# Attention and MLP layers on one core: the second attention's q and k by seven block products, and its fillers in a new order

## The chip, the cores and the metric

The kernel runs on one core of a Trainium2 chip. The metric is the device time of one launch in microseconds (us), inputs and outputs in device memory.

## The reference

Sixteen images of 256 channels and 1024 pixels, all in float32, pass through two layers:

```python
# layer 0: 4 heads of 64
qkv = xs @ w_proj + b_proj
x   = xs + softmax(q k^T / 8) v @ w_out + b_out
# layer 1: group norms, 8 heads of 32, MLP with 1024 hidden units
n   = group_norm(x, gn1)
q, k, v = n @ qkv_w.T                      # no bias
x   = x + softmax(q k^T / sqrt(32) + phys_bias) v @ proj_w.T + proj_b
h   = group_norm(x, gn2)
x   = x + gelu(h @ mlp_w1.T + b1) @ mlp_w2.T + b2
```

## The kernel before

The images run one after the other, in a pipeline over neighbours. For image b the loop in `first_pass` does four things:

- **First attention** (`attention_a`, lines 425 to 503): 32 steps of scores `s_a`, exponential `e_a` on ScalarE, weighting `acc_a`, and sums `es_a` of the exponentials on VectorE.
- **The gap between the attentions**: the `hidden` pieces of image b-1, that is the MLP's first product (lines 957 to 1019: `begin`, `middle`, `finish` for four pairs of hidden blocks), with the output projection `o` and the group norm `gn_g` of image b mixed in by a list of due times (`Later`). Then the first four of the eight q/k products of the second layer (`qk_b`, line 357, copied out by ScalarE in line 832) and the first of its four v products (`v_b`).
- **Second attention** (`attention_b`, lines 563 to 620): 16 steps, 0 to 15. A step makes scores `s_b` for two key blocks of four heads, exponentials `e_b` (line 578), weights the step before (`acc_b`, line 607), adds the exponentials up on VectorE (`es_b`, line 591), and adds `acc_b` into `res_b` (line 620; ScalarE's line 618 in a group's first step). After each step PE gets **fillers**, which a dictionary `fill` assigns by step: the other v and q/k products of this image (`own`), the seven products of the MLP's second part of image b-1 (`outputs`, `m<-g`), and the q, k and v products of the first layer for image b+1 (`first`: `qk_a` and `v_a`). A step's full filler is 3.4 us of PE work: one output, or two of the small pieces.
- **Storing**: after an MLP output the results are added up on VectorE (lines 1074, 1078), and blocks are combined for the products that follow (line 1019).

The MLP is already computed by seven block products in place of eight (a Strassen-like scheme); its sums of weights are made once, kept in device memory and loaded for each image.

TensorE's products are float32, so a 128x128 by 128x512 product shows as two records. PSUM has eight banks: three "wide" pairs (`wide`, taken in turn, the least recently used first) and two single ones (`bank` 0 and 1). A step's scores take all eight. The weighting takes bank 0 again, which the next step's scores want first. Eight buffers `e` hold exponentials and other temporary tiles. The order of each engine's instructions is fixed when the program is built.

In the second attention of images 1 to 14 the fillers before are: steps 0 to 2 an own v and an own q/k product each; step 3 the last own q/k product and the first of `first`; steps 4 to 15 one output or two of `first`; after step 15 the last of `first`. The output projection `j` of the second attention's first half falls into step 14.

Of the kernel before, what the change touches and what calls it, by code (L numbers as in the profile page):

```python
# [8 lines left out]
F32 = mybir.dt.float32  # L9
# [5 lines left out]
P = 128  # L15
# [4 lines left out]
TB = 512  # L20
# [239 lines left out]
def first_pass(ctx, tc, x, out, k):  # L260
    nc = tc.nc
    B, C, S = x.shape
    CC, SB, NT = C // P, S // P, S // TB
    HC = k["m1b"].shape[1]
    later = Later()

    act = ctx.enter_context(tc.tile_pool(name="act", bufs=1))
    work = ctx.enter_context(tc.tile_pool(name="work", bufs=2))
# [8 lines left out]
    dram = ctx.enter_context(  # L277
        tc.tile_pool(name="dram", bufs=4, space=bass.MemoryType.DRAM)
    )
# [26 lines left out]
    def use(n):  # L306
        order.remove(n)
        order.append(n)

    def wide(name, n=None):  # L310
        if n is None:
            n = next(m for m in order if m not in kept)
        use(n)
        return ps_s.tile([P, 2, TB], F32, tag=f"s{n}", name=name)

    def bank(name, n):
        return ps_a.tile([P, TB], F32, tag=f"b{n}", name=name)


    aside = []  # L320
# [33 lines left out]
    def product(o, w, r, **flags):  # L354
        for c0 in range(0, P, cols[0]):
            sl = slice(c0, c0 + cols[0])
            nc.tensor.matmul(o[sl], w[:, sl], r, **flags)  # L357
# [391 lines left out]
    def group_norm(key, src, stats, gw, gb, tag, out_tile, wait, then=None):  # L749
        st = {}  # L750

        def averages(name, src, apart):
            if cols[0] == P:
                ps = bank(name, 1)
                product(ps[:, :CC], k["gavg"], src, start=True, stop=True)
                return [(slice(0, P), ps[:, :CC])]
            if apart:
                ps = [bank(f"{name}_{n}", n) for n in range(2)]  # L760
            else:
                both = wide(name)
                ps = [both[:, n, :] for n in range(2)]
            halves = [slice(h, h + HALF) for h in range(0, P, HALF)]
            for n, sl in enumerate(halves):
                nc.tensor.matmul(
                    ps[n][sl, :CC], k["gavg"][sl, sl], src[sl], start=True, stop=True
                )
            return [(sl, ps[n][sl, :CC]) for n, sl in enumerate(halves)]

        def means():
            mv = small.tile([P, CC, 2], F32, tag="mv", name=f"mv_{key}")
            for cc in range(CC):
                nc.vector.bn_aggr(mv[:, cc, :], stats[:, cc].rearrange("p t k -> p (t k)"))
            mean_c = small.tile([P, CC], F32, tag="mean_c", name=f"mean_c_{key}")
            nc.vector.tensor_copy(mean_c, mv[:, :, 0])
            st.update(mv=mv, mean_c=mean_c)
            later.after(wait, variances)

        def variances():  # L780
            mean = small.tile([P, CC], F32, tag="mean", name=f"mean_{key}")
            for sl, ps in averages(f"gm_{key}", st["mean_c"], True):
                nc.vector.tensor_copy(mean[sl], ps)

            dv = small.tile([P, CC], F32, tag="dv", name=f"dv_{key}")
            nc.vector.tensor_sub(dv, st["mean_c"], mean)
            nc.vector.tensor_mul(dv, dv, dv)
            nc.vector.tensor_add(dv, dv, st["mv"][:, :, 1])
            st.update(mean=mean, tv=dv)
            later.after(1 if cols[0] == P else 5, apply)  # L790

        def apply():
            rstd = small.tile([P, CC], F32, tag="rstd", name=f"rstd_{key}")
            for sl, ps in averages(f"gv_{key}", st["tv"], False):
                nc.vector.tensor_scalar(rstd[sl], ps, EPS, None, ALU.add)
            nc.gpsimd.tensor_tensor(rstd, rstd, k["mhalf"], ALU.pow)
            a = rstd
            nc.vector.tensor_mul(a, rstd, gw)
            ma = small.tile([P, CC], F32, tag="gma", name=f"gma_{key}")
            nc.vector.tensor_mul(ma, st["mean"], a)  # L800
            c = ma
            nc.vector.tensor_sub(c, gb, ma)
            y = act.tile([P, CC, S], F32, tag=tag, name=f"gn_{key}")
            out_tile.append(y)
            for t in range(NT):
                sl = slice(t * TB, (t + 1) * TB)
                for cc in range(CC):
                    nc.vector.tensor_scalar(
                        y[:, cc, sl], src[:, cc, sl],
                        a[:, cc : cc + 1], c[:, cc : cc + 1], ALU.mult, ALU.add,  # L810
                    )
            if then:
                then(y)

        means()
# [106 lines left out]

    inputs = {}

    def sums_of_input(b, y):
# [165 lines left out]
    def run(stage, fill=None):  # L1093
        for n, _ in enumerate(stage):
            pieces = fill.get(n, ()) if fill else ()
            if n > last:
                run_pieces(pieces, False)
            later.tick()
            if n <= last:
                run_pieces(pieces, False)  # L1100

    def run_pieces(pieces, tick=True):
        for piece in pieces:
            piece()
            if tick:
                later.tick()
# [9 lines left out]
    xs = {0: load_x(0)}  # L1116
# [4 lines left out]
    ps, n = bank("bqk", 0), brow.shape[0]  # L1121
# [4 lines left out]
    start = first_qk[::2] + first_qk[1::2] + first_v  # L1126
# [5 lines left out]
    for m in (1, 2):  # L1132
        made = act.tile([P, 7, TB], F32, tag="ws", name=f"w{m}_made")
# [17 lines left out]
    later.after(2, fold_bias)  # L1151
    later.after(8, k["scale_v"])
    later.after(9, k["fold_ones"])
    hidden, outputs = [], []
    last = NT * CC * SB // 2 - 1
    for b in range(B):
        def load_next(b=b):
            if not b:
                xs[1] = load_x(1)
                return  # L1160
            with tc.issue_after(spread_out["last"].ins):
                load_blocks(1, b - 1)
                if b + 1 < B:
                    xs[b + 1] = load_x(b + 1)

        later.after(14, load_next)
        xn = []
        run(
            attention_0(
                b, tiles0, xs[b],  # L1170
                lambda st, b=b, xn=xn: group_norm(
                    f"g{b}", xs[b], st, k["g1w"], k["g1b"], "res", xn, 2 if b else 3
                ),
            )
        )
        first = []
        if b + 1 < B:
            tiles0, (first_qk, first_v) = qkv_0(b + 1, xs[b + 1])
            first = first_qk + first_v
        run_pieces(first if b == 0 else hidden)  # L1180
        later.flush()
        if b:
            load_blocks(2, b - 1)
        if b == B - 1:
            load_blocks(1, b, True)
        tiles1, (qk, v) = qkv_1(b, xn[0])
        n = len(qk) // CC

        aside.extend((1, 0))
        run_pieces(qk[:n] + v[:1])
        def early(piece):
            aside.append(0)
            piece()

        own = [lambda: early(v[1]), qk[n], v[2], qk[n + 1], v[3], *qk[n + 2 :]]
        fill = {m: own[2 * m : 2 * m + 2] for m in range((len(own) + 1) // 2)}
        now, end = outputs, []
        if b == 0:  # L1200
            first = []
        if b == B - 1:

            now, end = outputs[:3], outputs[3:]
        if not first:

            fill = {m: [piece] for m, piece in enumerate(own[:5:2] + own[1::2] + own[6:])}
            fill.update({len(own) + 3 * m: [piece] for m, piece in enumerate(now)})
            now = []

        rest = [[piece] for piece in now]
        at = len(fill)
        if first:
            fill[at - 1] = fill[at - 1] + first[:1]
            fill[last + 1] = first[-1:]
            for m, at_most in enumerate((1, 4, 6, 8, 10)):
                rest.insert(at_most, first[2 * m + 1 : 2 * m + 3])
        for m, pieces in enumerate(rest):
            fill[at + m] = pieces
        hn = []  # L1220
        run(
            attention_1(
                b, tiles1, xs[b],
                lambda st, b=b, hn=hn: group_norm(
                    f"h{b}", xs[b], st, k["g2w"], k["g2b"], "q1", hn,
                    *((3 if b + 1 < B else 1), lambda y, b=b: sums_of_input(b, y)),
                ),
            ),
            fill,
        )  # L1230
        run_pieces(end)
        hidden, outputs = mlp(b, xs[b])
# [13 lines left out]
    both = small.tile([P, 1], F32, tag="part", name="both")  # L1246
# [295 lines left out]
```

## Time and profile before

| what | us |
|---|---|
| median of 3 runs (3643.26 to 3645.5) | 3643.72 |
| the profiled execution's own time | 3643.38 |
| its span, first to last instruction | 3641.6 |
| TensorE busy | 3615.4 |
| VectorE busy | 2667.9 |
| ScalarE busy | 2132.0 |
| one image from start to start (image 7 to 8: 1565.2 to 1789.5) | 224.3 |
| of it first attention, gap, second attention, end | 60.3, 41.5, 120.0, 2.5 |

PE is TensorE's matmul row, PEld its weight loads, DVE VectorE, ACT ScalarE, POOL GpSimd, SP the queue engine that issues most DMAs. A timeline row gives start, duration, engine, line, operation, output and inputs, and how many instructions were merged into it; in brackets the idle time before it and what ended it. The granted TensorE clock was 0.999 of full speed.

### The profile page before, as it was taken

To read this page: it belongs to the slowest core of one execution; us is meant where nothing else is said; L and a number is where in the kernel's file an instruction comes from. 1 tells how busy PE (TensorE), PEld (TensorE's weight loads), DVE (VectorE), ACT (ScalarE), POOL (GpSimd) and SP (SyncE) were. 2 spreads that over 40 slices of the span, in tenths; PEclk is the share of its full clock that TensorE was granted. 3 is DMA by queue.
4 is the path that set the end of the run, shared out by engine and by line. 5 is a ranking of instruction groups with operands and counts; after the bars stand their busy time and mean duration, and the time that the engine had idled before them with its cause. 6 is when DMAs were issued, how large, how long until landed. Compare 5 with 4: busy or idle time off the path is not lost.

```text
span 3641.6 us, 80411 instructions
## 1 busy us (share of the span) xinstructions
PE 3615.4 (99%) x34557; PEld 1353.1 (37%) x34557; DVE 2667.9 (73%) x3440; ACT 2132.0 (59%) x2833; POOL 215.0 (6%) x317
## 2 busy tenths in 40 slices
PE   9999999999999999999999999999999999999998
PEld 3433343333433334343343333434334343343433
DVE  4586777767777677777777777777776777767787
ACT  4665656556565655656556565565655656556572
POOL 4000000000000000000000000000000000000000
PEclk9999999999999999999999999999999999999999
DMA  3011212213121131211212122121221212212100
GB/s 117 10 48 39 62 51 39 60 39 80 33 48 51 39 80 33 51 53 40 74 33 51 54 49 64 33 51 54 51 63 39 46 53 54 66 37 48 58 27 25
DMA packets 79409, 182.48 MB, mean 50 GB/s; under 512 B 37734, under 2 KB 38502, under 8 KB 74822
## 3 DMA queue, kind: packets, MB, share of 16 engines
q1 hardware_dynamic: 69668, 148.66, 13.6%
q0 software_dynamic: 7632, 28.21, 5.0%
q8 instruction: 272, 4.46, 0.5%
q10 hardware_dynamic: 1746, 0.40, 0.1%
q14 instruction: 91, 0.75, 0.1%
HBM read 111.17 MB, written 21.23 MB: 36 GB/s over the span
## 4 chain that ended last, share of the span: by engine, by line
PE 91%; DVE 5%; DMA 2%; issue 1%; ACT 1%; SPq 0%; ACTq 0%; POOL 0%; DVEq 0%
PE s_b L563 13%; PE s_a L425 12%; PE acc_b L607 12%; PE acc_a L446 12%; PE m L357 10%; PE m L957 7%; PE qk_a L357 6%; PE qk_b L357 6%; PE v_a L357 3%; PE v_b L357 3%; PE j L357 3%; PE o L357 2%; DVE g L1019 1%; PE den_a L479 1%; DMA d_a<-row_a 1%
## 5 line engine op out<-in xcount | busy, mean ns | idle before, releaser
L578 ACT ACTIVATE e_b<-s_b 128x1024 f32<-128x1024 f32 (+1 forms) x1280 | 982.8, 864 | 164.2 <-PE s_b L563 164.2
L591 DVE TENSOR_TENSOR es_b<-es_b,e_b 128x1024 f32<-128x1024 f32 x768 | 899.6, 1220 | 242.8 <-ACT e_b L578 241.5
L433 ACT ACTIVATE e_a<-s_a 128x1024 f32<-128x1024 f32 x512 | 521.3, 1025 | 360.2 <-PE s_a L425 348.4
L425 PE MATMUL s_a<-q,k 64*64 64x512 f32 x4096 | 544.2, 593 | 0.0
L446 PE MATMUL acc_a<-e_a,v 64*64 64x512 f32 x4096 | 540.1, 589 | 0.0
L460 DVE TENSOR_TENSOR es_a<-es_a,e_a 128x1024 f32<-128x1024 f32 x384 | 473.8, 1234 | 71.1 <-ACT e_a L433 50.6
L563 PE MATMUL s_b<-q,k 32*64 32x512 f32 x8192 | 521.4, 600 | 3.8 <-DVE res_b L620 1.6
L607 PE MATMUL acc_b<-e_b,v 128*32 128x512 f32 x4096 | 492.1, 598 | 0.0
L357 PE MATMUL m<-g,w 128*32 128x512 f32 (+1 forms) x3320 | 404.3, 592 | 0.0
L563 PEld LDWEIGHTS s_b<-q,k 32*64 32x64 f32 x8192 | 170.3, 130 | 321.6 <-issue 130.9
L446 PEld LDWEIGHTS acc_a<-e_a,v 64*64 64x64 f32 x4096 | 187.9, 133 | 251.5 <-issue 215.1
L425 PEld LDWEIGHTS s_a<-q,k 64*64 64x64 f32 x4096 | 175.9, 133 | 246.7 <-issue 204.9
L957 PE MATMUL m<-gn_h,w 128*128 128x512 f32 x512 | 243.7, 604 | 7.5 <-DVE g L983 4.9
L607 PEld LDWEIGHTS acc_b<-e_b,v 128*32 128x32 f32 x4096 | 108.5, 109 | 357.5 <-ACT e_b L578 194.7
L357 PE MATMUL qk_a<-x,wp 128*32 128x512 f32 (+1 forms) x1856 | 235.4, 593 | 3.6 <-ACT k L834 3.6
L357 PE MATMUL qk_b<-gn_g,wq 128*32 128x512 f32 (+1 forms) x1280 | 234.1, 592 | 0.0
L620 DVE TENSOR_TENSOR res_b<-res_b,acc_b 128x512 f32<-128x512 f32 x192 | 131.6, 686 | 125.3 <-PE acc_b L607 125.3
L357 PEld LDWEIGHTS m<-g,w 128*32 128x32 f32 (+1 forms) x3320 | 121.2, 112 | 253.9 <-issue 226.6
L1019 DVE TENSOR_TENSOR g<-g,g 128x512 f32<-128x512 f32 x320 | 206.7, 678 | 3.9 <-ACT g L970 2.8
L591 DVE TENSOR_TENSOR es_b<-e_b,e_b 128x1024 f32<-128x1024 f32 x128 | 150.6, 1217 | 52.4 <-ACT e_b L578 52.4
L957 PE MATMUL m<-hs,w 128*128 128x512 f32 x384 | 177.9, 592 | 0.1
L970 ACT ACTIVATE g<-g,m1b 128x512 f32<-128x512 f32 x128 | 91.7, 721 | 102.2 <-DVE g L999 75.5
(154 smaller groups left out, 2870.6 us busy)
## 6 DMA issues: line engine op xcount, KB each, us to landing
w<-w_kept SPq DMA_DIRECT2D x30, 1792.0 KB
packed_b<-es_b SPq DMA_DIRECT2D x42, 512.0 KB
packed_b<-es_b POOLq DMA_DIRECT2D x42, 512.0 KB, 6.5
d_a<-row_a SPq DMA_DIRECT2D x64, 256.0 KB
rd_b<-row_b SPq DMA_DIRECT2D x252, 64.0 KB
out_dram<-x SPq DMA_DIRECT2D x63, 256.0 KB
x<-in_x_dram SPq DMA_DIRECT2D x30, 512.0 KB
w_kept<-w_made POOLq DMA_DIRECT2D x2, 1792.0 KB, 6.1
```

The costliest lines, as they stand in the source:

```text
L357: nc.tensor.matmul(o[sl], w[:, sl], r, **flags)
L425: nc.tensor.matmul(s[h : h + HALF, g, :], kT[g * D : (g + 1) * D, c, kb * P + h : kb * P + h + HALF], qT[g * D : (g + 1) * D, c, t * TB : ...
L433: nc.scalar.activation(e, s, AF.Exp, scale=float(D) ** -0.5)
L446: nc.tensor.matmul(accs[i][h][g * D : (g + 1) * D, :], v[h * HALF : (h + 1) * HALF, kb, c * 2 + g], e[h * HALF : (h + 1) * HALF, g, :], st ...
L460: nc.vector.tensor_add(sums[i], held[i] if kb == 1 else sums[i], e)
L563: nc.tensor.matmul(outs[g][h : h + HALF, :], kT[g * D : (g + 1) * D, c, k0 : k0 + HALF], qT[g * D : (g + 1) * D, c, t * TB : (t + 1) * TB] ...
L578: nc.scalar.activation(to, s, AF.Exp, scale=float(D) ** -0.5)
L591: ins = nc.vector.tensor_add(d, es[n % 2] if kb == 0 else d, es[n])
L607: nc.tensor.matmul(acc[g * D : (g + 1) * D, :], v[:, kb + m, c * G + g], es[2 * m + g // 2][:, g % 2, :], start=(m == 0), stop=(m == 1),)
L620: nc.vector.tensor_add(r, r, acc)
L957: nc.tensor.matmul(ps, blocks[1][number - 1][:, i * P : (i + 1) * P], inputs[b][number], start=first, stop=True, skip_group_check=not first,)
L1019: (nc.vector.tensor_add if plus else nc.vector.tensor_sub)(d, d, gs[(*what, i)])
```

## The change

For images 1 to 14 (images 0 and 15 keep the eight products, and their fillers):

- q and k of the second layer come from seven products per channel half `ch` in place of eight. The two input halves and the two pixel halves are the blocks b11, b12, b21, b22; `sums_for_qk` makes four sums t1 to t4 of them on VectorE right after the group norm, in three buffers of kind `e` together with the weights' sums. Those are made once, in image 0's first attention (`make_qk_blocks`, 8 additions of 128x128), kept in device memory and loaded (512 KB) for each image.
- All 14 products run in the gap. Partial results are summed in PSUM: product 1 goes to one bank of a wide pair, ScalarE copies it into the other, and later products are added onto both; product 7 goes to a single bank, is copied to SBUF, and product 4 is added onto the bank.
- The first v product is placed ahead of the last of the 14, and takes a wide pair.
- The fillers are dealt out anew: step 0 v1 and v2; step 1 v3 and the first of `first`; outputs in steps 2, 4, 5, 7, 9, 11 and 13; pieces of `first` in steps 3 (one), 6, 8, 10, 12 (two each) and 15 (one); step 14 nothing; after step 15 the last of `first`, as before.

```diff
+    def make_qk_blocks():
+        made = work.tile([P, 2, TB], F32, tag="e", name="qk7_made", bufs=8)
...
+            nc.vector.tensor_add(s1, a21, a22)
+            nc.vector.tensor_sub(s2, s1, a11)
+            nc.vector.tensor_sub(s3, a11, a21)
+            nc.vector.tensor_sub(s4, a12, s2)
+        nc.sync.dma_start(kept_qk, made)
...
+        def load():
+            t = work.tile([P, 2, TB], F32, tag="e", name=f"qk7_{b}", bufs=8)
...
+            nc.sync.dma_start(st["w"], kept_qk)
+
+        def sums(y):
...
+            nc.vector.tensor_sub(t3, b22, b12)
+            nc.vector.tensor_sub(t1, b12, b11)
+            nc.vector.tensor_sub(t2, b22, t1)
+            nc.vector.tensor_sub(t4, b21, t2)
...
+            def p1(ch):
+                both = wide(f"qk7_{b}_{ch}")
+                ps[ch] = both[:, 0, :], both[:, 1, :], bank(f"qk7y_{b}_{ch}", 1 - ch)
+                got[ch] = work.tile([P, 2, TB], F32, tag="e", name=f"qk7p_{b}_{ch}", bufs=8)
+                one, two, _ = ps[ch]
+                mm(one, qk_block(1, ch, 0), "b11", True)
+                nc.scalar.copy(two, one)
+
+            def p7(ch):
+                mm(ps[ch][2], st["w"][:, ch, 2], "t3", True)
+                nc.scalar.copy(got[ch][:, 0], ps[ch][2])
+
+            def p6(ch):
+                mm(ps[ch][1], st["w"][:, ch, 1], "t2", False)
+                nc.scalar.copy(got[ch][:, 1], ps[ch][1])
+
+            def p2(ch):
+                mm(ps[ch][0], qk_block(1, ch, 1), "b21", False)
+                nc.scalar.copy(half(kk, ch, 0), ps[ch][0])
+
+            def p4(ch):
+                mm(ps[ch][2], qk_block(0, ch, 1), "t4", False)
+                nc.vector.tensor_add(half(q, ch, 0), got[ch][:, 1], ps[ch][2])
+
+            def p5(ch):
+                mm(ps[ch][1], st["w"][:, ch, 0], "t1", False)
+                nc.vector.tensor_add(half(q, ch, 1), got[ch][:, 0], ps[ch][1])
+
+            def p3(ch):
+                mm(ps[ch][1], st["w"][:, ch, 3], "b22", False)
+                nc.scalar.copy(half(kk, ch, 1), ps[ch][1])
...
+                    (p1, 0), (p1, 1), (p7, 0), (p7, 1), (p6, 0), (p2, 0), (p6, 1), (p4, 0),
+                    (p5, 0), (p2, 1), (p4, 1), (p3, 0), (p5, 1), (p3, 1),
...
+    later.after(10, make_qk_blocks)
...
+        seven = 0 < b < B - 1
...
+        if seven:
+            load_qk()
...
-        aside.extend((1, 0))
-        run_pieces(qk[:n] + v[:1])
+        if seven:
+            made = qk_pieces(*tiles1[:2])
+            run_pieces(made[:-1] + v[:1] + made[-1:])
...
-        fill = {m: own[2 * m : 2 * m + 2] for m in range((len(own) + 1) // 2)}
...
         if first:
-            fill[at - 1] = fill[at - 1] + first[:1]
+            o = [[piece] for piece in now]
+            f = [first[1:2]] + [first[n : n + 2] for n in range(2, 10, 2)]
+            fill = dict(enumerate((
+                [own[0], v[2]], [v[3], first[0]],
+                o[0], f[0], o[1], o[2], f[1], o[3], f[2], o[4], f[3], o[5], f[4], o[6],
+                [], first[10:11],
+            )))
             fill[last + 1] = first[-1:]
-            for m, at_most in enumerate((1, 4, 6, 8, 10)):
-                rest.insert(at_most, first[2 * m + 1 : 2 * m + 3])
```

More of the change, by code (lines that the diff above doesn't have):

```diff
@@ L915, in attention_1, with qk_block @@
         return attention_b(b, q, kk, v, project)
+    kept_qk = dram.tile([P, 2, 4, P], F32, tag="qk7", name="qk7_kept", bufs=1)
+    def qk_block(which, ch, cc):
+        at = which * C + ch * P
+        return k["wq"][:, cc, at : at + P]
+    def make_qk_blocks():
+        made = work.tile([P, 2, TB], F32, tag="e", name="qk7_made", bufs=8)
+        made = made.rearrange("p c (n m) -> p c n m", m=P)
+        for ch in range(CC):
+            a11, a12 = (qk_block(1, ch, cc) for cc in range(CC))
+            a21, a22 = (qk_block(0, ch, cc) for cc in range(CC))
+            s1, s2, s3, s4 = (made[:, ch, n] for n in range(4))
+            nc.vector.tensor_add(s1, a21, a22)
[3 more added lines that the diff above has]
+        nc.sync.dma_start(kept_qk, made)
@@ new lines, in qk_by_seven, with pieces, half, mm @@
+    def qk_by_seven(b):
+        st, ps, got = {}, {}, {}
+        def load():
+            t = work.tile([P, 2, TB], F32, tag="e", name=f"qk7_{b}", bufs=8)
+            st["w"] = t.rearrange("p c (n m) -> p c n m", m=P)
+            nc.sync.dma_start(st["w"], kept_qk)
+        def sums(y):
+            two = [
+                work.tile([P, 2, TB], F32, tag="e", name=f"qk7t_{b}_{n}", bufs=8)
+                for n in range(2)
+            ]
+            b11, b12 = (y[:, 0, t * TB : (t + 1) * TB] for t in range(NT))
+            b21, b22 = (y[:, 1, t * TB : (t + 1) * TB] for t in range(NT))
+            t1, t2 = (two[0][:, n] for n in range(2))
+            t3, t4 = (two[1][:, n] for n in range(2))
+            nc.vector.tensor_sub(t3, b22, b12)
+            nc.vector.tensor_sub(t1, b12, b11)
+            nc.vector.tensor_sub(t2, b22, t1)
+            nc.vector.tensor_sub(t4, b21, t2)
+            st.update(t1=t1, t2=t2, t3=t3, t4=t4, b11=b11, b21=b21, b22=b22)
+        def pieces(q, kk):
+            def half(d, ch, t):
+                return d[:, ch, t * TB : (t + 1) * TB]
+            def mm(to, w, x, first):
+                nc.tensor.matmul(
+                    to, w, st[x], start=first, stop=True, skip_group_check=not first
+                )
+            def p1(ch):
[23 more added lines that the diff above has]
+                nc.scalar.copy(half(kk, ch, 1), ps[ch][1])
+            return [
+                lambda p=p, ch=ch: p(ch)
+                for p, ch in (
+                    (p1, 0), (p1, 1), (p7, 0), (p7, 1), (p6, 0), (p2, 0), (p6, 1), (p4, 0),
+                    (p5, 0), (p2, 1), (p4, 1), (p3, 0), (p5, 1), (p3, 1),
+                )
+            ]
+        return load, sums, pieces
@@ L1167, in first_pass @@
         xn = []
+        seven = 0 < b < B - 1
+        load_qk, sums_for_qk, qk_pieces = qk_by_seven(b)
         run(
@@ L1170, in first_pass @@
                 b, tiles0, xs[b],
-                lambda st, b=b, xn=xn: group_norm(
-                    f"g{b}", xs[b], st, k["g1w"], k["g1b"], "res", xn, 2 if b else 3
+                lambda st, b=b, xn=xn, seven=seven, then=sums_for_qk: group_norm(
+                    f"g{b}", xs[b], st, k["g1w"], k["g1b"], "res", xn, 2 if b else 3,
+                    then if seven else None,
                 ),
@@ L1187, in first_pass @@
         n = len(qk) // CC
-        aside.extend((1, 0))
-        run_pieces(qk[:n] + v[:1])
+        if seven:
+            made = qk_pieces(*tiles1[:2])
+            run_pieces(made[:-1] + v[:1] + made[-1:])
+        else:
+            aside.extend((1, 0))
+            run_pieces(qk[:n] + v[:1])
         def early(piece):
@@ L1209, in first_pass @@
             now = []
-        rest = [[piece] for piece in now]
-        at = len(fill)
         if first:
-            fill[at - 1] = fill[at - 1] + first[:1]
+            o = [[piece] for piece in now]
[5 more added lines that the diff above has]
+            )))
             fill[last + 1] = first[-1:]
-            for m, at_most in enumerate((1, 4, 6, 8, 10)):
-                rest.insert(at_most, first[2 * m + 1 : 2 * m + 3])
-        for m, pieces in enumerate(rest):
-            fill[at + m] = pieces
         hn = []
```

## The prediction

> **What bounds the kernel now.** I read the engine sums first, then the chain of waits, then stretches of one inner image (number 7; images 1 to 14 repeat every 224.4 us), then the timelines at the places that the change touches.
>
> From the profile page:
>
> ```profile
> PE 3615.4 (99%) x34557; PEld 1353.1 (37%) x34557; DVE 2667.9 (73%) x3440; ACT 2132.0 (59%) x2833; POOL 215.0 (6%) x317
> ...
> PE 91%; DVE 5%; DMA 2%; issue 1%; ACT 1%; SPq 0%; ACTq 0%; POOL 0%; DVEq 0%
> ```
>
> TensorE bounds the kernel, so work taken from it should count in full. But "busy" is not "never waits". The PE timeline of image 0, where the steps of the second attention from 167 us on have no filler, shows it:
>
> ```profile
> 161.79 1.98 PE L563 MATMUL s_b<-q,k 32*64 32x512 f32 x32
> ...
> 167.27 1.97 PE L563 MATMUL s_b<-q,k 32*64 32x512 f32 x32
> ...
> 171.02 3.12 PE L563 MATMUL s_b<-q,k 32*64 32x512 f32 x32
> ```
>
> The same 32 matmuls take 1.97 us, or 3.12 when they wait for banks that ScalarE and VectorE empty: waits hide inside busy spans. Starts of `s_b` give a step's length: 5.48 us with half a filler (161.79 to 167.27), 3.75 with none after a filled one (167.27 to 171.02). A full filler makes 7.19 (1694.05 to 1701.24 in image 7).
>
> Busy time by stretch, image 7: first attention, gap between the attentions, second attention (columns: us, then PE, PEld, DVE, ACT, POOL):
>
> ```profile
> 1565.20:1625.50 60.30, 60.30 (x576) 24.73 (x576) 46.87 (x62) 35.17 (x37) 3.13 (x5) 1.00 0.22 72
> 1625.50:1667.00 41.50, 41.34 (x144) 18.37 (x145) 27.19 (x51) 19.19 (x29) 1.15 (x3) 1.00 0.17 58
> 1667.00:1787.00 120.00, 120.00 (x1461) 39.45 (x1464) 91.35 (x101) 78.18 (x110) 8.03 (x9) 1.00 0.21 39
> ```
>
> VectorE has slack on average in each (27 of 41 us, 91 of 120), so only its order against PE can hurt.
>
> **What is taken out.** PE, end of the gap:
>
> ```profile
> 1658.29 7.03 PE L357 MATMUL qk_b<-gn_g,wq 128*128 128x512 f32 x16
> 1665.15 1.89 PE L357 MATMUL v_b<-wq,gn_g 128*128 128x256 f32 x8
> 1666.97 1.97 PE L563 MATMUL s_b<-q,k 32*64 32x512 f32 x32
> ```
>
> Eight 128x512 products (two records each) take 6.86 us, 0.857 each. An image now makes q and k with 16 products, 8 here and 8 as fillers; after the change 14, all here. The built order of both kernels agrees: 14 per image on PE. The gap gets 6 x 0.857 = +5.14. The second attention loses four half fillers: step 3 becomes half (7.19 to 5.48, -1.71), step 14 empty (7.19 to 3.75, -3.44; in image 7 it also holds `j` and a small `den_b`, 4.0 us, both kept), step 15 half (-1.71): -6.86. Net -1.72 an image, -24.0 over 14 images. That is the most the change can bring.
>
> **What it adds beside PE.** Per image VectorE gets four 128x512 sums of the input (0.68 each, like L1019) and four additions into q (0.68, like L465), and ScalarE's four copies of q give way to six of partial results (its four of k stay). All lie in the gap. I walked the built order with the durations above; three waits follow.
>
> *Wait A, in the gap.* VectorE:
>
> ```profile
> 1655.28 1.92 DVE L808 TENSOR_SCALAR gn_g<-x,rstd_g,gma_g 128x512 f32<-128x512 f32 x4
> 1657.11 0.68 DVE L999 TENSOR_TENSOR g<-g,m 128x512 f32<-128x512 f32 x1
> 1657.82 0.69 DVE L1000 TENSOR_TENSOR g<-g,m 128x512 f32<-128x512 f32 x1
> ```
>
> After `gn_g` (1657.20) the new order is t3, t1, L999, t2, L1000, t4, at 0.60 from start to start (L1019 x2 take 1.29). L1000, which frees the first wide pair of banks, ends at 1660.31, not 1658.51. PE runs product 1 of half 1 and product 7 of half 0 from 1658.29 to 1660.00, then product 1 of half 0 waits for that pair: 0.36. Its result is copied by ScalarE into the second bank, behind two gelus and two other copies (0.72 and 0.59 each, like L970 and L832): done 1662.09, product 6 due 1662.07: 0.07. Product 3 waits for an addition into q: 0.09. Sum 0.52. The other relays have over 2 us. A PSUM-to-PSUM copy stands nowhere in the trace; the nearest rows are 0.57 (shortest L832) and 1.04 (L578 at 128x1024, twice the elements). I take 0.59, as L832 has the same shape and source; each 0.1 more moves product 6 by up to 0.3 (three such copies stand in the queue), below 0.59 only the 0.07 can go.
>
> *Wait B, step 4.* The first MLP output moves from step 4 to step 2, so its VectorE additions fall into step 3, now the short one. The same eight instructions stand in step 10 of image 7:
>
> ```profile
> 1737.83 2.49 DVE L1019 TENSOR_TENSOR g<-g,g 128x512 f32<-128x512 f32 x4
> 1740.24 1.29 DVE L1078 TENSOR_TENSOR x<-x,lent 128x512 f32<-128x512 f32 x2
> 1741.44 1.22 DVE L591 TENSOR_TENSOR es_b<-es_b,e_b 128x1024 f32<-128x1024 f32 x1
> 1742.58 0.68 DVE L620 TENSOR_TENSOR res_b<-res_b,acc_b 128x512 f32<-128x512 f32 x1
> ```
>
> They take 5.43 us, and L620 frees the bank into which the next step's scores go first. Step 10 lasts over 7.19: no wait. In step 3 they begin when VectorE has ended step 2's additions, in image 7 at 1684.16 + 3.49 - 1679.66 = 7.99 us after step 2's scores, less 0.07 of overlap, and end at 13.35; the scores of step 4 are due at 7.19 + 5.48 = 12.67. With 0.05 for the semaphore: 0.73. Behind the waiting scores stands all of PE.
>
> *Wait C, step 15.* PE, then VectorE:
>
> ```profile
> 1771.03 3.62 PE L357 MATMUL j<-res_b,wpj 128*32 128x512 f32 x32
> 1774.47 3.64 PE L357 MATMUL v_a<-wp,x 128*32 128x256 f32 x64
> 1778.03 1.97 PE L563 MATMUL s_b<-q,k 32*64 32x512 f32 x32
> ```
>
> ```profile
> 1771.45 3.49 DVE L591 TENSOR_TENSOR es_b<-es_b,e_b 128x1024 f32<-128x1024 f32 x3
> 1774.86 1.41 DVE L722 SCALAR_TENSOR_TENSOR x<-j,pjb,x 128x512 f32<-128x512 f32 x2
> ```
>
> Without the `v_a` pieces here the scores start at 1774.60, and their last wide pair, needed 1.28 later (1775.88), is the one that `j` used; VectorE lets go of it at 1776.27 + 0.05. 0.44. After it the chain holds: step 15's last additions end 0.7 us before `den_b` asks for them.
>
> **The rest.** The weight sums are made once, in image 0: eight 128x128 additions, by 0.23 (L190, 128x128) to 0.38 (L225, 128x256) 1.8 to 3.0 us of VectorE near 50 us, where it idles 0.3 to 0.5 us in each later step: 0, at most 2. Their 512 KB load per image stands on SP behind `d_a<-row_a` (1606.49) and ahead of `sp_a<-d_a` (1628.90); the e buffer that it waits for is the first of the last eight, free over 10 us before that. The same 512 KB of `d_a<-row_a` move in about 3 us (1607.7 to 1610.5); the load is needed at 1659, so 0; without that cover, about 3 us an image. The MLP weights (issued 1658.48, all of it moved by 1666) are wanted in step 2, near 1689, not at 1697.70: still over 20 us after landing, so 0.
>
> **Sum.** Per image -1.72 + 0.52 + 0.73 + 0.44 = -0.03; times 14, -0.4. The profiled execution took 3643.38 us (span 3641.6 and 1.8 around it; the median of the runs shown is 3643.72): 3643.0. About 0.2%, 7.3 us (0.52 an image), is what a measurement of this kernel can tell from no change.
>
> **One rule of the skill, weighed.** The row: in image 0's 3.12 us above, scores wait for one bank and nothing passes them. The Trainium skill, "PSUM — Partial Sum Buffer", section "Engine vs sequencer instructions", says that ScalarE and VectorE queues are strict FIFO and matmuls start and complete in program order. It speaks against the change: by it waits B and C are not filled by later products, and the sum stays -0.03 an image; were they passed, it would be -1.20. Another page, "ScalarE: Activation LUTs", section "Step-by-step: what each stage is for", says that ScalarE writes PSUM with lower latency than SBUF; no row here shows it, and by it the relay's 0.07 would go.
>
> **Rivals.** (1) *Faster: A and C are not there.* Both are differences of about 0.4 us between walked times; if VectorE reaches L1000 and the two `j` additions that much sooner, 0.96 an image comes back: -13.8 against 3643.38, 3629.5. For it: VectorE's slack in both stretches. Against: the order is built so, and the `j` additions stood right behind L591 already. (2) *Slower: ScalarE's relay.* Product 6 of half 0 waits for the fifth of five ScalarE instructions (three copies and two gelus). If copies within PSUM last 0.9 us, not 0.59, it waits some 0.9 more: +12.6, 3655.6. It decides from 0.77 us a copy (0.18 x 3 = 0.55 above my sum). For it: no row has such a copy. Against: L832's 0.59. (3) *The change doesn't do what it says*: excluded by the built order, 14 products an image. (4) *No waits at all*: 3619.4; B alone, the best founded, speaks against it.
>
> **How the numbers follow.** Waits give the gain back, within 0.2%: 0.40 (own range 3636 to 3651). Rival 1, or a part of it with B smaller: 0.30. Rival 2 or such waits elsewhere: 0.30. So faster 0.30, same 0.40, slower 0.30. The range takes in rival 1 (3629.5) with the 0.07 above it, and the upper bound of the copies, 1.04 us (3 x 0.45 x 14 = 18.9 over the sum): 3628 to 3662.
>
> **What would show it.** Right: 28 fewer full products; gap about 5.7 us longer (47.2), second attention about 5.7 shorter (114.3); the `s_b` span of step 4 and of step 15 longer than 1.97 or a gap ahead of them; product 1 of half 0 late by 0.4. Wrong: steps at 5.48 and 3.75 with no stretched `s_b` (rival 1), copies of 0.8 us and a hole before product 6 (rival 2), or a changed first attention.

## The result and the profile after

| what | before | after |
|---|---|---|
| median of five runs (us) | 3643.72 | 3658.71 |
| range of the runs | 3643.26 to 3645.50 | 3657.88 to 3661.55 |
| span of the profiled execution | 3641.6 | 3656.9 |
| one image, start to start (the commonest of images 1 to 14) | 224.34 | 225.73 |
| of it from the first `s_a` to the first `s_b` | 101.79 | 107.67 |
| of it from the first `s_b` to the next `s_a` | 122.55 | 118.05 |

The ratio is 1.0042, with a 95% interval of 1.0027 to 1.0057: 0.4% slower. 3643.0 had been forecast, no change; the time lies inside the range.

The page of after, with the engine sums and the chain of waits:

```profile
PE 3620.8 (99%) x33829; PEld 1352.0 (37%) x33829; DVE 2739.4 (75%) x3560; ACT 2140.2 (59%) x2861; POOL 198.6 (5%) x317
...
PE 82%; issue 10%; DVE 7%; ACT 1%; DMA 1%; POOL 0%; SPq 0%; ACTq 0%; DVEq 0%; POOLq 0%
```

TensorE has 728 records fewer and yet 5.4 us more busy time. (A q/k product shows as eight records where it is a filler and as two in the gap, so most of the records that are gone are not work that is gone.) The records of `s_b` are not longer one by one, 601 ns in the mean and 600 before. But together they cover 543.4 us, not 521.4: where a bank is late, records that would have run side by side follow one another, and the wait shows as busy time. On the chain of waits VectorE rises from 5 to 7%. PE falls from 91 to 82%, as "issue", time in which nothing that the profile shows was waited for, rises from 1 to 10%. That is no measure of the loss: one of the kernels below is quicker than before (3627.08 us) and has 9% of it. The waits of PE over the whole execution (what waited, for what; us in total, times, longest):

```profile
PE s_b L563 <- DVE res_b L620: 10.7, 16, 0.9
...
PE qk L972 <- DVE g L1093: 2.9, 14, 0.2
```

In before the first row was 1.6 us in 2 times, and the second did not exist. These are 14 images, once each. They are two of four places; the other two show only as a stretched `s_b`. Busy time by stretch of image 7: first attention, gap, second attention:

```profile
1572.10:1632.40 60.30, 60.30 (x576) 24.69 (x576) 46.90 (x62) 35.14 (x37) 2.82 (x5) 1.00 0.23 76
1632.40:1679.73 47.33, 46.96 (x153) 20.35 (x150) 32.95 (x60) 21.55 (x34) 1.14 (x3) 1.00 0.15 51
1679.73:1795.25 115.52, 114.86 (x1397) 37.42 (x1400) 89.69 (x99) 76.39 (x107) 6.59 (x8) 1.00 0.22 43
```

The first attention is unchanged. The gap was to take 47.2 and takes 47.33; the second attention was to take 114.3 and takes 115.5. So most of the error lies in the second attention. The starts of `s_b` in image 7 give the steps' lengths, 0 to 14:

```
before  5.49 7.20 7.20 7.19 7.19 7.19 7.63 7.19 7.19 7.19 7.63 7.19 7.20 7.19 11.20
after   5.49 7.20 7.19 6.20 7.19 7.19 7.63 7.19 7.19 7.19 7.63 7.19 7.92 7.19  7.74
```

Step 3 is a half step but lasts 6.20 in place of 5.48 (wait B). Step 12 lasts 0.72 more, which the prediction did not have: wait D. Step 14 is shorter by 3.46, as forecast. Wait C falls into step 15, behind the last start.

*A, the gap.* PE of after:

```profile
1666.02 1.02 PE L972 MATMUL qk7y<-qk7t,qk 128*128 128x512 f32 x2
1667.24 1.13 PE L972 MATMUL qk<-gn_g,wq 128*128 128x512 f32 x2 [0.21 <-DVE g L1093]
```

Product 1 of half 0 starts 1.22 us after product 7, not 0.86: 0.36, as walked, behind VectorE's L1093 (L1000 in before). It also lasts 1.13, not 1.02: the interval from its first record to its second is 0.53 us, not 0.43. From the first `s_a` to the first `s_b` there are 5.88 us more; less the 5.14 of the products, A is 0.74.

*B, step 3 to 4.* PE, then VectorE:

```profile
1703.25 1.90 PE L357 MATMUL qk_a<-x,wp 128*32 128x512 f32 x16
1705.81 1.98 PE L563 MATMUL s_b<-q,k 32*64 32x512 f32 x32 [0.66 <-DVE res_b L620]
```

```profile
1700.33 0.68 DVE L1112 TENSOR_TENSOR g<-g,g 128x512 f32<-128x512 f32 x1
1700.93 1.29 DVE L1171 TENSOR_TENSOR x<-x,lent 128x512 f32<-128x512 f32 x2
1702.13 0.69 DVE L1112 TENSOR_TENSOR g<-g,g 128x512 f32<-128x512 f32 x1
1702.73 1.22 DVE L591 TENSOR_TENSOR es_b<-es_b,e_b 128x1024 f32<-128x1024 f32 x1
1703.87 1.29 DVE L1112 TENSOR_TENSOR g<-g,g 128x512 f32<-128x512 f32 x2
1705.07 0.68 DVE L620 TENSOR_TENSOR res_b<-res_b,acc_b 128x512 f32<-128x512 f32 x1
```

The eight instructions run from 1700.33 to 1705.75 (5.42; 5.43 were walked), and the scores start 0.06 later.

*C, step 15.* PE, then VectorE:

```profile
1783.51 3.62 PE L357 MATMUL j<-res_b,wpj 128*32 128x512 f32 x32
1787.06 2.92 PE L563 MATMUL s_b<-q,k 32*64 32x512 f32 x32
```

```profile
1787.34 1.40 DVE L722 SCALAR_TENSOR_TENSOR x<-j,pjb,x 128x512 f32<-128x512 f32 x2
```

The scores take 2.92, not 1.97: 0.95. VectorE ends the `j` additions 1.68 us after the scores' start (1.67 were walked).

*D, step 12.* PE, then VectorE:

```profile
1764.21 2.68 PE L563 MATMUL s_b<-q,k 32*64 32x512 f32 x32
```

```profile
1761.52 3.49 DVE L591 TENSOR_TENSOR es_b<-es_b,e_b 128x1024 f32<-128x1024 f32 x3
1764.92 0.24 DVE L384 RECIPROCAL inv_b<-sp_b 128x16 f32<-128x16 f32 x1
1765.09 0.66 DVE L1167 SCALAR_TENSOR_TENSOR x<-m,m2b,x 128x512 f32<-128x512 f32 x1
```

The sixth MLP output, in step 11, is one of the two that VectorE takes straight out of its bank (L1167), while ScalarE copies the first five out. It stands behind three `es_b` additions and a reciprocal, ends 1.54 us after the scores began, and its pair is their third: 2.68 - 1.97 = 0.71, in the steps' lengths 0.72. In before this output stood in step 13, where the scores of step 14 took 2.09.

The four waits and the net gain make -1.72 + 0.74 + 0.72 + 0.95 + 0.72 = +1.41 an image; 225.73 - 224.34 = 1.39 was measured. Times 14 that is 19.5, the spans differ by 15.3. The rest lies outside the four waits: three gaps of before (images 5, 9, 13) are 0.6 to 1.6 us longer than its others, one of after is (image 14, 1.3), a difference of 2.5; the stretch ahead of image 0's first `s_a` is 0.6 shorter in after, and single second attentions of before are longer than their median, 1.1 in all. In the long gap of image 9 VectorE waits 5.53 us for the transfer `d_a<-row_a`, in that of image 7 it waits 3.54. Whether the change has a part in such late transfers is not shown.

### The profile page after: what moved, and what is told of

The parts are those of the page before. It is cut to its first block, busy times and chain, and to the rows that moved or that the text cites. A ratio compares the mean times of both kernels' runs of the same rounds, so it can differ in the third digit from the quotient of the medians.

```text
span 3656.9 us, 79215 instructions
## 1 busy us (share of the span) xinstructions
PE 3620.8 (99%) x33829; PEld 1352.0 (37%) x33829; DVE 2739.4 (75%) x3560; ACT 2140.2 (59%) x2861; POOL 198.6 (5%) x317
## 4 chain that ended last, share of the span: by engine, by line
PE 82%; issue 10%; DVE 7%; ACT 1%; DMA 1%; POOL 0%; SPq 0%; ACTq 0%; DVEq 0%; POOLq 0%
PE s_b L563 13%; PE s_a L425 12%; PE acc_a L446 12%; PE acc_b L607 11%; PE m L357 9%; PE qk_a L357 5%; PE qk L972 3%; PE v_a L357 3%; PE v_b L357 3%; PE j L357 3%; PE m L1050 2%; PE o L357 2%; DVE es_b L591 2%; PE qk7y L972 1%; PE den_a L479 1%
## 5 line engine op out<-in xcount | busy, mean ns | idle before, releaser
L563 PE MATMUL s_b<-q,k 32*64 32x512 f32 x8192 | 543.4, 601 | 13.0 <-DVE res_b L620 10.7
L620 DVE TENSOR_TENSOR res_b<-res_b,acc_b 128x512 f32<-128x512 f32 x192 | 130.7, 681 | 102.1 <-PE acc_b L607 102.1
L460 DVE TENSOR_TENSOR es_a<-e_a,e_a 128x1024 f32<-128x1024 f32 x64 | 78.4, 1225 | 108.0 <-ACT e_a L433 107.9
```

The costliest lines, as they stand in the source:

```text
L460: nc.vector.tensor_add(sums[i], held[i] if kb == 1 else sums[i], e)
L563: nc.tensor.matmul(outs[g][h : h + HALF, :], kT[g * D : (g + 1) * D, c, k0 : k0 + HALF], qT[g * D : (g + 1) * D, c, t * TB : (t + 1) * TB] ...
```

## The experiments

Theory 1: the work is as cheap as forecast, and the loss is four waits for banks that the order alone sets. The rival: the products or VectorE's additions are dear in themselves, so a wait taken away comes back elsewhere. Every kernel below was timed in five rounds against the kernel before; period is what an undisturbed one of images 1 to 14 takes from start to start (before 224.34, after 225.73). Two things blur the totals and not the periods. After was not timed again, and before took 3644.2 and 3644.5 us beside these kernels, not 3643.72. And the stretch ahead of image 0's first `s_a`, into which none of the edits below reaches, takes 30.8 to 35.0 us in the ten traces.

**B taken out**: steps 2 and 3 change fillers.

```diff
-                o[0], f[0], o[1], o[2], f[1], o[3], f[2], o[4], f[3], o[5], f[4], o[6],
+                f[0], o[0], o[1], o[2], f[1], o[3], f[2], o[4], f[3], o[5], f[4], o[6],
```

> The fillers of steps 2 and 3 change places: step 2 gets the single piece of first, step 3 the first MLP output. The work is the same. Theory 1 (the changed kernel is slow by four waits for PSUM banks, each set by the order alone): the additions behind the first output then fall into a full step, s_b of step 4 starts on time, 0.72 us an image goes, 14 x 0.72 = 10.1: 3658.7 - 10.1 = 3648.6 us. Rival (the products and their added VectorE and PSUM work are dearer in themselves, so that a wait which is taken away comes back at the next shared bank): within 3 us of 3658.7, with the 0.7 us found again in a later step of the same image.

Measured: 3649.78, ratio 1.0015 [1.0006, 1.0024]; period 224.99, down by 0.74. The scores of this step start on time, and later steps keep their lengths (step 12 still 7.92):

```profile
1698.35 3.62 PE L357 MATMUL m<-g,w 128*32 128x512 f32 x32
1701.90 1.97 PE L563 MATMUL s_b<-q,k 32*64 32x512 f32 x32
```

The rival fails here.

**D taken out**: the output moves from step 11 to 12.

```diff
-                o[0], f[0], o[1], o[2], f[1], o[3], f[2], o[4], f[3], o[5], f[4], o[6],
+                o[0], f[0], o[1], o[2], f[1], o[3], f[2], o[4], f[3], f[4], o[5], o[6],
```

> The sixth output and the last two pieces of first change places, so that the output stands in step 12 and not in step 11, whose bank VectorE empties behind three es_b additions. The work is the same. Theory 1: s_b of step 12 falls from 2.68 to 1.97 us; a wait of up to 0.1 may stay at step 13; 0.6 to 0.7 us an image goes, 8.4 to 10: about 3649 us. Rival: the wait of 0.7 us turns up in full at step 13, total within 3 us of 3658.7.

Measured: 3651.78, ratio 1.0018 [1.0009, 1.0027]; period 225.03, down by 0.70. In image 7 `s_b` of step 12 is back at 1.97, and of step 13 it is 2.03: a wait of 0.06 stays, as expected. But in four images (7 among them, with 2.50 us for `s_b` of step 14) 0.3 to 0.5 comes back: there VectorE waits in step 13 for a transfer, as in the next experiment. The total fell by 6.9, where 8.4 to 10 were expected.

**C taken out**: half a filler in step 14.

```diff
-                o[0], f[0], o[1], o[2], f[1], o[3], f[2], o[4], f[3], o[5], f[4], o[6],
-                [], first[10:11],
+                o[0], f[0], o[1], o[2], f[1], o[3], f[2], o[4], f[3], o[5], f[4][:1], o[6],
+                f[4][1:], first[10:11],
```

> One of the two pieces of first in step 12 moves to step 14, behind the projection j; step 12 becomes a half step, step 14 gets 1.71 us more. The work is the same. Theory 1: s_b of step 15 starts 1.7 us later than the j additions need, falls from 2.92 to 1.97 us, and 0.95 us an image goes: 13.3, about 3645.4 us; if the half step 12 now makes step 13 wait for VectorE, less. Rival: the wait comes back at step 13 or at the end of the attention, total within 3 us of 3658.7.

Measured: 3656.26, ratio 1.0031 [1.0020, 1.0042]; 2.5 us below after, within the rival's 3. The images differ here, from 224.85 to 226.38; their mean is 225.51, in after 225.83, down by 0.32 only, and the stretch ahead of image 0 is the longest of all, 35.0. `s_b` of step 15 is back at 1.97, so C is gone; but step 14 lasts 9.46 to 10.79 in different images, where 9.45 was due. Image 5, PE, then VectorE:

```profile
1327.23 1.95 PE L563 MATMUL s_b<-q,k 32*64 32x512 f32 x24
1329.56 1.09 PE L563 MATMUL s_b<-q,k 32*64 32x512 f32 x8 [0.37 <-DVE x L1167]
```

```profile
1328.15 0.69 DVE L682 TENSOR_TENSOR res_b<-res_b,rd_b 128x512 f32<-128x512 f32 x1 [1.23 <-DMA rd_b<-row_b]
1328.76 0.74 DVE L1167 SCALAR_TENSOR_TENSOR x<-m,m2b,x 128x512 f32<-128x512 f32 x1
```

A new wait: VectorE stands still for 1.23 us until a transfer of the reciprocals lands. L1167, whose product PE has ended by 1327.3, stands behind it, and the last eight records of `s_b` behind L1167. In 11 of the 14 images L682 waits so, by 0.1 to 1.2 us; in after it waits here in none. Step 12 is now 1.7 us shorter, so PE and VectorE come to step 13 that much sooner after its transfers were issued. This is the Trainium skill's "PSUM — Partial Sum Buffer", section "Engine vs sequencer instructions", in a trace: VectorE's queue is strict FIFO, so the waiting instruction holds up the one behind it, here by up to 1.23 us.

**The same, with L1167 ahead of L682.** In step 13 the fillers are issued before what is due.

```diff
-            if n > last:
+            if n > last or n == 13:
                 run_pieces(pieces, False)
             later.tick()
-            if n <= last:
+            if n <= last and n != 13:
```

> The kernel with the half filler in step 14, and in step 13 VectorE empties the bank of the last MLP output (L1167) ahead of the product res_b<-res_b,rd_b (L682) and not behind it. L682 waits for a transfer of the reciprocals that takes its own time, and in the short step 12 it came 0.1 to 1.2 us late in half of the images, with L1167 and the scores of step 14 behind it. Theory 1: step 13 then ends without a wait in all images, the whole 0.95 us of wait C is gone: 3658.7 - 13.3 = 3645.4 us, second attention 114.5 in every image. Rival (the scores of step 14 are late for another reason, the wait stays): 3655 us as with the half filler alone, second attention 114.6 to 115.9.

Measured: 3645.61, ratio 1.0004 [0.9995, 1.0013]; period 224.73, down by 1.00, and the second attention lasts 114.5 in every image. VectorE in image 7:

```profile
1770.50 0.75 DVE L1167 SCALAR_TENSOR_TENSOR x<-m,m2b,x 128x512 f32<-128x512 f32 x1 [0.46 <-PE m L357]
1771.17 0.68 DVE L682 TENSOR_TENSOR res_b<-res_b,rd_b 128x512 f32<-128x512 f32 x1
```

One exchange on VectorE's queue is worth some 10 us: 10.7 between the medians (3656.26 to 3645.61), 9.1 in images 1 to 14 of the two traces. C's full price is recovered, and the rival fails.

**B and D together.**

```diff
-                o[0], f[0], o[1], o[2], f[1], o[3], f[2], o[4], f[3], o[5], f[4], o[6],
+                f[0], o[0], o[1], o[2], f[1], o[3], f[2], o[4], f[3], f[4], o[5], o[6],
```

> Both swaps together: the single piece in step 2 and the first output in step 3; two pieces in step 11 and the sixth output in step 12. Theory 1: the waits B and D are separate, the gains add up: 3658.7 - 9.5 - 8 = about 3641 us. Rival: one wait covers the other in part, 3646 us or more.

Measured: 3640.80, ratio 0.9989 [0.9980, 0.9998]; period 224.30, down by 1.43; alone they gave 0.74 and 0.70. The two add up. In three images the wait for the transfer comes back here too (0.3 to 0.6).

**A made smaller**: another order of the 14 products, fixed by `issue_after`, with the banks taken in the old order.

```diff
-                    (p1, 0), (p1, 1), (p7, 0), (p7, 1), (p6, 0), (p2, 0), (p6, 1), (p4, 0),
-                    (p5, 0), (p2, 1), (p4, 1), (p3, 0), (p5, 1), (p3, 1),
+                    (p1, 1), (p7, 0), (p7, 1), (p1, 0), (p6, 1), (p6, 0), (p4, 0), (p2, 0),
+                    (p2, 1), (p4, 1), (p5, 0), (p5, 1), (p3, 0), (p3, 1),
...
-            run_pieces(made[:-1] + v[:1] + made[-1:])
+            run_pieces(made[:-2] + v[:1] + made[-2:])
```

> The 14 products in the gap are put into another order, with product 1 of half 0 fourth, so that its wide pair has 1.7 us more to come free; product 6 of both halves and product 3 of half 0 get more time behind their copies and additions. The work is the same. Theory 1: of the 0.75 us of waits in the gap some 0.6 goes, 8.4 us: about 3650 us. Rival: the waits move to other products of the 14, gap 47.4 us as before it, total within 3 us of 3658.7.

Measured: 3656.88, ratio 1.0036 [1.0022, 1.0049]; period 225.46, down by 0.27, less than half of what was expected. The total is 1.8 below after, within the rival's 3 us, and the rival is half right: some of the wait has moved. Product 1's wait is gone; single records (each matmul's own start) show 0.27 us of a new one ahead of product 2 of half 0, which starts 0.05 us after ScalarE's copy of the other bank of its pair.

**The dealing of before, the seven products kept.** What the q/k fillers leave is taken out of steps 1 to 3 and of step 14.

```diff
-                [own[0], v[2]], [v[3], first[0]],
-                o[0], f[0], o[1], o[2], f[1], o[3], f[2], o[4], f[3], o[5], f[4], o[6],
-                [], first[10:11],
+                [own[0], v[2]], [v[3]], first[:1], first[1:2],
+                o[0], first[2:4], o[1], o[2], first[4:6], o[3], first[6:8], o[4],
+                first[8:10], o[5], first[10:11], o[6],
```

> The seven products stay; the dealing of before comes back from step 4 on, but for one piece of first that step 14 loses. What the four q/k fillers leave is taken out of steps 1 to 3 (one small piece each) and of step 14 (one piece behind j). Theory 1: steps 4 to 13 last as in the kernel before, waits B, C and D are not there, only A (0.75 us an image) stays: per image -1.72 + 0.75 = -0.97, 14 x -0.97 = -13.6: 3630 us, gap 47.4, second attention 113.2. Rival (the products are dear in themselves and waits only move): the short steps 1 to 3, in which VectorE needs 5.3 of 5.48 us, give new waits, total 3643 us or more.

Measured: 3627.08, ratio 0.9952 [0.9939, 0.9966]; period 223.35, 2.38 below after and 0.99 below before (0.97 expected; in the total, 17.4 us below before where 13.6 was expected, the three long gaps of before make most of the rest). Gap 47.4, second attention 113.2. In image 7 steps 1 to 3 last 5.49, 5.48 and 5.47: VectorE keeps up. The scores of step 15, behind `j` and half a filler:

```profile
1765.79 3.62 PE L357 MATMUL j<-res_b,wpj 128*32 128x512 f32 x32
1769.22 1.91 PE L357 MATMUL v_a<-wp,x 128*32 128x256 f32 x32
1771.06 1.97 PE L563 MATMUL s_b<-q,k 32*64 32x512 f32 x32
```

Of PE's waits for L620 only the two of before are left:

```profile
PE s_b L563 <- DVE res_b L620: 1.6, 2, 0.9
```

So the same products, with every addition that they bring, make the kernel 0.5% faster than before. The dealing alone made the change slower.

**The same with the gap's order**, product 2 of half 0 one place later. The lines with a minus are the order of the gap experiment above.

```diff
-                    (p1, 1), (p7, 0), (p7, 1), (p1, 0), (p6, 1), (p6, 0), (p4, 0), (p2, 0),
-                    (p2, 1), (p4, 1), (p5, 0), (p5, 1), (p3, 0), (p3, 1),
+                    (p1, 1), (p7, 0), (p7, 1), (p1, 0), (p6, 1), (p6, 0), (p4, 0), (p2, 1),
+                    (p2, 0), (p4, 1), (p5, 0), (p5, 1), (p3, 0), (p3, 1),
```

> The same dealing, and the 14 products in an order like that of the gap experiment, with product 2 of half 0 one place later, because it waited there 0.27 us for ScalarE's copy out of the same pair of banks. Theory 1: the gap falls from 47.4 to 46.7 to 46.9 us, 0.5 to 0.7 an image: 7 to 10 under the dealing alone, about 3622 us. Rival: gap 47.1 as in the first gap experiment or longer, at most 4 us under the dealing alone.

Measured: 3622.29, ratio 0.9940 [0.9926, 0.9953]; period 223.00, the best of all: 0.6% faster than before, 1.0% than after. The time came as said; the gap did not quite: 47.0, and 4.8 us under the dealing alone, where 7 to 10 were expected. Of A 0.39 is left (107.32 - 101.79 - 5.14), by single records mainly three stretches of 0.10 to 0.17 at product 6 and around the first v product. That rest was not followed further.

## Why the prediction was wrong

- **The gain, -1.72 an image: right.** With the waits taken away, 223.00 and 223.35 against 224.34 leave only what is left of A.
- **A, 0.52: measured 0.74.** The wait on VectorE is 0.36, as walked. By single records product 1 and product 3 of half 0 each lose 0.10 more between their first and second record (0.53 us, not 0.43), which the sum lacked; the waits at product 6 and product 3 are 0.07 and 0.09, as walked.
- **B, 0.73: measured 0.72** (6.20 - 5.48), and 0.74 when taken out. The best founded term held.
- **C, 0.44: measured 0.95. A term of the sum was mis-sized.** That VectorE would let go of `j`'s pair 1.72 us after the scores' start was right (1.73 with 0.05 for the semaphore). Wrong was "needed 1.28 later". Single records of an unhindered `s_b` (step 15 of the kernel with the exchanged L1167) show four groups of eight records that start at 0, 0.48, 0.91 and 1.34: the third pair is already written by half of the third group, at 0.91, and 1.28 is nearly the start of the fourth. 1.73 - 0.91 is 0.82. In after the groups come at the same times with eight, eight, four and four records; the other four and four follow only at 1.83, 0.10 after the bank was free, and at 2.28. 1.83 - 0.91 is 0.92, nearly all of the 0.95. Two pairs of heads that would have run side by side ran one after the other.
- **D: not in the sum at all, 0.72.** The step that failed is "I walked the built order ...; three waits follow". The new place of the sixth output, whose bank VectorE empties and not ScalarE, was not walked. By 1.28 it would have shown 0.31 (1.54 + 0.05 - 1.28); by 0.91 it shows 0.68, and the late records do start at 1.59.
- **"VectorE has slack on average in each ... so only its order against PE can hurt": right.** It was 75% busy in the slowest kernel and 76% in one of the two quickest (2740.4 us of 3625.3), and in the experiments the order alone, with the same work, is worth up to 36 us (3658.71 to 3622.29).
- **Rival 1** (A and C absent) and **rival 4** (no waits) did not come about. **Rival 2** fell: the copies within PSUM (L982) take 0.574 us in the median. The Trainium skill, "ScalarE: Activation LUTs", section "Step-by-step: what each stage is for", has ScalarE write PSUM with lower latency than SBUF; here the difference in duration is hardly there: L990, from PSUM to SBUF in the same shape, takes 0.578.

A sum whose terms nearly cancel (-1.72 and +1.69) has no better sign than its worst term; two errors of 0.5 and 0.7 us an image, in the same direction, made 17 us, and A's 0.2 another 3; some 4 us outside the four waits went the other way, so the time missed by 15.7. That it lies inside the range all the same is in part luck: the upper end was taken from slow copies (rival 2), and those did not come.

## What to carry to other kernels

When fillers are dealt out anew, each shared bank has a date at which its emptier is done and a date at which the next product wants it; both have to be walked for every step that moved, by which engine empties the bank and what stands ahead on that engine's queue. Take the date of need from single records of an unhindered step, and for the first group of records that writes the bank, not for the last. And if removed work brings nothing, try the same work in the old order before giving it up: here 3658.7 and 3622.3 us hold the same products.

## What was not expected of the hardware

- A late bank can split matmuls that run side by side: at step 15 the eight records of the third group, which in an unhindered step start within 0.05 us, start as four and four, 0.92 us apart (0.91 and 1.83), and no idle time shows.
- In the gap a product behind a wait restarts slowly: the interval between its two records is then 0.53 us, not 0.43 (products 1 and 3 of half 0 in after).
- A transfer that was in time can become a wait on PE through VectorE's queue when PE gets there sooner: VectorE waits up to 1.23 us, different from image to image.
